# A Mamba-2 stage whose decay matrix is made from running sums that DMA broadcasts, in place of masked matrix products

## The chip, the cores and the metric

The kernel runs on one core of one Trainium2 chip. A core has five engines with instruction queues of their own: TensorE (PE, with its weight loads shown apart as PEld), VectorE (DVE), ScalarE (ACT), GpSimd (POOL) and SyncE (SP), which here issues nearly all DMA transfers. The metric is device time in microseconds (us) of one execution; a measurement of this kernel can tell a difference of about 0.2% from none.

## The reference

The reference is two transformer-like layers on x of 4 rows x 512 tokens x 512 channels, in float32. Each of four blocks first gates x with a bidirectional decaying sum over a side input (the "gates"; they depend on the side input and the condition, not on x, so they can be made ahead), then adds the block's output to x: a Mamba-2 mixer, a mixture of 8 experts (top 2), grouped attention with 16 heads, and a gated feed-forward with 1408 hidden channels.

The change lies in the Mamba-2 mixer. Cut to what matters, with 16 heads and a step size dt per token and head:

```python
dt = softplus(zxbcdt[..., -16:] + dt_bias)
dA = dt * (-exp(A_log))                      # negative, per token and head
dA_cs = cumsum(dA, axis=-1)                  # within a chunk of tokens
seg = dA_cs[..., :, None] - dA_cs[..., None, :]
Lmat = where(tri, exp(seg), 0.0)             # decay from token s to token l, l >= s
Y_diag = einsum('bcgls,bgHcls,bcsgHp->bclgHp', CB, Lmat, xdt)
decay_states = exp(dA_cs[..., -1:] - dA_cs)
Y_off = einsum('bclgn,bcgHpn,bgHcl->bclgHp', Cc, prev, exp(dA_cs))
```

After that follow a skip term, a gate silu(z), a root-mean-square norm and an output projection. The chunk length doesn't change the result; the kernel takes 128 tokens.

## The kernel before

Everything is float32. The stages run one after another: the first gates; the Mamba stage for the rows b = 0 to 3, in which the gates for later blocks and the routing of the experts are made as well; the experts; attention; the feed-forward. Instructions are written in one program order, and a scheduler of the framework orders each engine's queue from it; once built, each engine runs its queue strictly in order. `after(...)` holds back some instructions in that scheduling.

**A row of the Mamba stage** (from `start_row`, L961). `start_scan` computes dt and dA for the row's 512 tokens (`time_steps`, L865, a chain of small VectorE instructions with 64 columns: 4 tiles x 16 heads) and the B and C channels; `more_x` computes the other eight chunks of channels (`conv_chunk`, L915: four products on PE into one bank, one pass on ACT, three on VectorE). The next row's are made in tiles 2 and 3 of the row before. Then four tiles of 128 tokens follow.

**A tile** is put together by the loop at L1219. `start_tile` makes z (L994, 16 PE records of 512 columns) and its silu. `start_scores` (L1006) multiplies the tile's dA by three constant matrices (L1011: `tri_le` gives running sums, `tri_gt` the sums that are still to come, `ones` the total), takes exponentials of the 48 columns (`ex`), makes C times B (`cb`, masked with `tri_le` by VectorE, L1020) and a transpose of B (`bt`). `decays(u, hh)` (L1028) is called once for each half of the 16 heads. For each four heads it forms r, `tri_le` scaled by each head's dA: one GpSimd instruction for the first four (L1036), four ACT instructions for the other four (L1044). One product of `tri_gt` with r (L1046, `pseg`) then gives, for every pair of tokens, the sum of dA between them; ACT takes its exponential (`lm`, L1050) and VectorE multiplies by `cb` (L1051). The function also transposes x, scales it with dt (`xdt`) and with `dte` (`xde`), and starts the skip term. `outputs` (L1076) multiplies `lm` with `xdt` (L1087), adds the part from the state and updates the state. `squares`, `norm`, `turn`, `project`, `scale` and `add_x` finish the tile one tile later; `norm` is three Newton steps on one column, on GpSimd (L1128 to L1131).

**Gates in between.** `pump` (L367) moves a generator (`make_gates`, L337) some steps forward at about seven places of each tile. Each pair of channel chunks takes scans forward and backward on VectorE (L254, L260), with a product on ACT between them (`f`, L256), three VectorE passes (L271 to L275), and loads and stores on SP: `kt` (L235), `ek` (L240, L242), `ekv` (L244, L250), the finished gate `g` (L328). The buffer of a `kt` is free once L273 has read it. `apply_gate` (L375) and the routing of the experts (`route`, L488; its PE products at L512 and L555) take scratch tiles of a tag `th` with two buffers.

**Buffers.** `lm` has four buffers of four heads, r two, `cb` two. PE's results go to three tags of PSUM banks: `mm` (four), `tp` (two), `acc` (two); `pseg` takes an `mm`. At the start, before the first tile, some of these buffers are lent to the first gates.

## Time and profile before

| what | value |
|---|---|
| median of four runs | 2668.1 us (2663.76 to 2670.64) |
| profiled execution, its own time | 2674.81 us |
| its span, first to last instruction | 2673.1 us |
| busy: PE, DVE, ACT, POOL | 2514.9, 1434.4, 1004.3, 286.2 us |
| mean granted clock of PE | 0.974 |
| instructions | 24889 |

The profile is of one execution. An engine's busy time is the union of its instructions; records of PE overlap, as they are pipelined, so a mean duration of 600 ns is more than the time from one start to the next. A 512-column product in float32 appears as two records. PEclk is the clock that PE was granted, 1.00 being full speed. Waits say which engine sat idle before which line, until what ended it; "SPq" is SP's queue of DMA issues. By the lines in the profile, the first gates take 0 to about 60 us, the Mamba stage reaches from there to some 720 us (its tiles begin at 84 us), the experts end near 1240 us, and attention near 2210 us.

### The profile page before, as it was taken

The numbers are of one execution on the slowest core, as the hardware profiler recorded it, in microseconds if no ns is written. First come the engines' busy times: TensorE is split into PE (matmuls) and PEld (weight loads), VectorE is DVE, ScalarE is ACT, GpSimd is POOL, SyncE is SP. The second block draws the span as 40 slices with busy tenths as digits, with TensorE's granted clock in tenths as the row PEclk, the third lists the DMA queues.
The fourth block names the chain that finished last, engine by engine and source line by source line (L and its number), as shares of the span: only waits on it lengthen the run. The fifth ranks groups of instructions, "written<-read, shape, count | busy, mean of one in ns | idle before, by whom it ended". The sixth has DMA issues, their size and how long they took to land.

```text
span 2673.1 us, 24889 instructions
## 1 busy us (share of the span) xinstructions
PE 2514.9 (94%) x8398; PEld 1335.2 (50%) x8398; DVE 1434.4 (54%) x2777; ACT 1004.3 (38%) x2044; POOL 286.2 (11%) x403
## 2 busy tenths in 40 slices
PE   3999999999998999995999999999999999999999
PEld 1555555646644444442555555555555554444444
DVE  8788888896524565553675564555454441010110
ACT  4556545546321333331554544444444341010000
POOL 1141332223211112110000000000000000000000
PEclk9889899999999999997999999999999999999999
DMA  6121312212134487876120211111000003000000
GB/s 210 44 68 56 130 40 82 96 59 82 64 134 168 174 308 289 345 291 211 56 87 25 63 32 34 43 46 32 16 9 24 32 27 119 16 0 16 8 8 16
DMA packets 86111, 237.95 MB, mean 89 GB/s; under 512 B 9184, under 2 KB 18528, under 8 KB 75872
## 3 DMA queue, kind: packets, MB, share of 16 engines
q1 hardware_dynamic: 77440, 211.71, 22.9%
q0 software_dynamic: 6240, 20.45, 2.1%
q10 hardware_dynamic: 2304, 4.20, 0.4%
q8 instruction: 67, 1.10, 0.2%
q14 instruction: 60, 0.49, 0.1%
HBM read 268.05 MB, written 46.92 MB: 118 GB/s over the span
## 4 chain that ended last, share of the span: by engine, by line
PE 46%; DVE 4%; ACT 2%; DMA 1%; issue 1%; SPq 0%; POOLq 0%; ACTq 0%; DVEq 0%
PE pd L1521 8%; PE pq L1457 7%; PE pfu L1588 6%; PE pfo L1598 6%; PE pfg L1583 6%; PE pctx L1506 5%; PE psc L1474 3%; PE pv L1443 2%; PE ptp L1497 2%; PE pk L1435 2%; DVE nmax L1479 1%; DMA rr<-rows_o 1%; ACT pr L1484 1%; DVE psc L1477 1%; DVE den L260 0%
## 5 line engine op out<-in xcount | busy, mean ns | idle before, releaser
L1457 PE MATMUL pq<-h,wq 128*128 128x512 f32 x512 | 250.3, 605 | 7.5 <-ACT pr L1484 7.4
L1521 PE MATMUL pd<-cx,wd 128*128 128x512 f32 x512 | 222.4, 592 | 0.0
L923 PE MATMUL pc<-h,wxb 128*128 128x512 f32 x320 | 144.7, 610 | 37.7 <-DVE h L1199 37.7
L1593 DVE SCALAR_TENSOR_TENSOR hd<-pfu,cols,hd 128x512 f32<-128x512 f32 x44 | 33.0, 750 | 269.3 <-PE pfu L1588 269.2
L1477 DVE TENSOR_TENSOR psc<-psc,mask 128x128 f32<-128x128 f32 x256 | 71.9, 288 | 189.3 <-PE psc L1474 189.3
L1592 ACT ACTIVATE hd<-pfg,cols 128x512 f32<-128x512 f32 x44 | 30.2, 687 | 381.0 <-PE pfg L1583 381.0
L1484 ACT ACTIVATE pr<-psc,nmax 128x128 f32<-128x128 f32 (+3 forms) x256 | 135.1, 529 | 98.3 <-DVE nmax L1479 97.4
L1506 PE MATMUL pctx<-pT,v 128*128 128x512 f32 (+3 forms) x512 | 152.8, 441 | 7.3 <-ACT pT L1500 3.9
L1588 PE MATMUL pfu<-h,ffu 128*128 128x512 f32 x352 | 158.7, 592 | 0.9 <-DMA ffu<-in_upT 0.9
L1583 PE MATMUL pfg<-h,ffg 128*128 128x512 f32 x352 | 158.6, 592 | 0.0
L1521 PEld LDWEIGHTS pd<-cx,wd 128*128 128x128 f32 x512 | 96.1, 190 | 114.8 <-issue 110.5
L1474 PE MATMUL psc<-kT,qT 128*128 128x128 f32 (+3 forms) x512 | 151.4, 435 | 0.9 <-ACT pr L1484 0.7
L1598 PE MATMUL pfo<-hd,ffd 128*128 128x512 f32 x352 | 151.7, 592 | 0.0
L757 PE MATMUL po<-w,yT 128*128 128x512 f32 x312 | 141.6, 594 | 3.9 <-ACT yT L750 2.1
L724 PE MATMUL pg<-w,hT 128*128 128x512 f32 x312 | 141.6, 594 | 1.9 <-DMA w<-in_w1x 1.9
L1506 PEld LDWEIGHTS pctx<-pT,v 128*128 128x128 f32 x512 | 93.0, 189 | 96.8 <-issue 35.0
L735 PE MATMUL pn<-w,hT 128*128 128x512 f32 x312 | 140.4, 592 | 0.0
L1529 DVE TENSOR_TENSOR xr<-xr,pd 128x512 f32<-128x512 f32 x64 | 44.0, 688 | 174.8 <-PE pd L1521 174.8
L1479 DVE TENSOR_REDUCE nmax<-psc 128x1 f32<-128x128 f32 (+3 forms) x256 | 123.7, 485 | 2.7
L1497 PEld LDWEIGHTS ptp<-ident,pr 128*128 128x128 f32 x640 | 78.2, 143 | 86.8 <-issue 40.1
L994 PE MATMUL pz<-wzt,h 128*128 128x512 f32 x256 | 121.1, 614 | 0.0
L1457 PEld LDWEIGHTS pq<-h,wq 128*128 128x128 f32 x512 | 88.0, 194 | 66.1 <-issue 57.6
(292 smaller groups left out, 4314.0 us busy)
## 6 DMA issues: line engine op xcount, KB each, us to landing
w<-in_w1x SPq DMA_DIRECT2D x80, 1024.0 KB
w<-in_w2x SPq DMA_DIRECT2D x40, 1024.0 KB
wb<-in_b1x SPq DMA_DIRECT2D x40, 512.0 KB
kt<-in_fT SPq DMA_DIRECT2D x62, 256.0 KB
ek<-ek SPq DMA_DIRECT2D x62, 256.0 KB
ekv<-ekv SPq DMA_DIRECT2D x62, 256.0 KB
g<-num SPq DMA_DIRECT2D x30, 512.0 KB
h<-g SPq DMA_DIRECT2D x11, 1024.0 KB
```

Of the source, the lines that this page charges most:

```text
L724: nc.tensor.matmul(pg, lhsT=hT[:, k, :], rhs=self.w1[s][0][:, k, :], start=(k == 0), stop=(k == NC - 1))
L757: nc.tensor.matmul(po, lhsT=yT[:, j, :], rhs=self.w2[s][:, j, :], start=(j == 0), stop=(j == NI - 1))
L923: nc.tensor.matmul(pc, lhsT=wxb[:, k, m * P : (m + 1) * P], rhs=h[:, k, :], start=(k == 0), stop=(k == NC - 1),)
L1457: nc.tensor.matmul(pq, lhsT=u.wq[:, k, i * KVC : (i + 1) * KVC], rhs=u.h[:, k, :], start=(k == 0), stop=(k == NC - 1),)
L1474: nc.tensor.matmul(psc[:, :n], lhsT=qT[:, qi * P : n], rhs=u.kT[:, :n], start=True, stop=True)
L1479: nc.vector.tensor_reduce(nmax, psc[:, :n], AX.X, ALU.max, negate=True)
L1484: nc.scalar.activation(pr, psc[:, :n], AF.Exp, bias=nmax, accum_out=rsum)
L1506: nc.tensor.matmul(pctx[:, kj * P :], lhsT=u.v[:, kj, :], rhs=pT[:, kj, kj * P :], start=(kj == 0), stop=(kj == NT - 1),)
L1521: nc.tensor.matmul(po, lhsT=u.wd[:, i, m * P : (m + 1) * P], rhs=u.ctxT[i], start=(i == 0), stop=(i == HPG - 1),)
L1583: nc.tensor.matmul(pg, lhsT=wg[:, k, cs], rhs=h[:, k, :], start=(k == 0), stop=(k == NC - 1))
L1588: nc.tensor.matmul(pu, lhsT=wu[:, k, cs], rhs=h[:, k, :], start=(k == 0), stop=(k == NC - 1))
L1598: nc.tensor.matmul(po, lhsT=wdn[:, i, m * P : (m + 1) * P], rhs=hd[i], start=(i == 0), stop=(i == NFF - 1),)
```

## The change

The decay between two tokens is made from the row's running sums, by differences.

- `time_steps` now makes the three kinds of sums for the whole row at once (three products of 64 columns, in a `tp` bank), their exponentials `ex`, `dte`, and a copy `cs` of the running sums. `cs` is transposed on PE, copied (`csT`: one row of 128 tokens for each tile and head) and stored in DRAM (`cs_d`). Its scratch columns are one `th` tile instead of tiles of their own.
- `load_sums(w, t, hh)` is new. A DMA on SP's queue reads the eight heads' running sums of a tile (4 KB) and writes them to all 128 partitions of an `lm` tile (512 KB). It is called once for each `decays`, about half a tile ahead of it in program order.
- `decays` works in that tile. Eight ACT instructions form max(0, cs of the partition's token - cs of the column's token), one per head; one ACT instruction takes exp(-that) over 1024 elements; VectorE multiplies by `cb` in two halves, as before. r, L1036, L1044 and `pseg` are gone. For pairs that `cb` masks the maximum makes the factor 1.
- `lm` has three buffers of eight heads, `cb` has one; the lending of buffers at the start follows. `norm` takes two GpSimd instructions in place of four for each Newton step; `squares` three in place of two.

The diff, without the lending of buffers and the renaming of scratch tiles:

```diff
+    cs_d = [dr.tile([NT * NH, P], F32, name=f"cs{b}") for b in range(B)]
...
@@ time_steps
+            four = tmp.tile([P, 4, n], F32, tag="th", name="dtv")
+            v, z, w, w2 = (four[:, i, :] for i in range(4))
...
-            dA = sm.tile([P, NT, NH], F32, tag="dA", name="dA", bufs=2)
+            dA = w2.rearrange("p (t h) -> p t h", h=NH)
             nc.vector.tensor_tensor(
                 dA, dt, negA.unsqueeze(1).to_broadcast([P, NT, NH]), ALU.mult
             )
-            return dt, dA
+
+            pp = ps_tp("ppr")
+            for i, m in enumerate((tri_le, tri_gt, ones)):
+                nc.tensor.matmul(
+                    pp[:, i * n : (i + 1) * n], lhsT=m, rhs=dA.rearrange("p t h -> p (t h)"),
+                    start=True, stop=True,
+                )
+            ex = sm.tile([P, 3, NT, NH], F32, tag="ex", name="ex", bufs=2)
+            act(ex.rearrange("p a t h -> p (a t h)"), pp[:, : 3 * n], AF.Exp)
+            dte = sm.tile([P, NT, NH], F32, tag="dte", name="dte", bufs=2)
+            nc.vector.tensor_tensor(dte, dt, ex[:, 1], ALU.mult)
+
+            cs = sm.tile([P, n], F32, tag="cs", name="cs", bufs=2)
+            nc.vector.tensor_copy(cs, pp[:, :n])
+            pcs = ps_tp("pcs")
+            nc.tensor.transpose(pcs[:n, :P], cs, ident)
+            csT = four[:n, 0:2, :].rearrange("p i t -> p (i t)")
+            nc.vector.tensor_copy(csT, pcs[:n, :P])
+            nc.sync.dma_start(out=cs_d[b], in_=csT)
+            return dt, cs, ex, dte
...
@@ start_scores
             pp = ps_tp("pp")
-            for i, m in enumerate((tri_le, tri_gt, ones)):
-                nc.tensor.matmul(
-                    pp[:, i * NH : (i + 1) * NH], lhsT=m, rhs=w.dA[:, t, :], start=True, stop=True
-                )
...
-            u.ex = sm.tile([P, 3, NH], F32, tag="ex", name="ex", bufs=2)
-            act(u.ex.rearrange("p a h -> p (a h)"), pp[:, : 3 * NH], AF.Exp)
-            u.cb = sm.tile([P, P], F32, tag="cb", name="cb", bufs=2)
+            u.cb = sm.tile([P, P], F32, tag="cb", name="cb")
...
-            u.dte = sm.tile([P, NH], F32, tag="dte", name="dte", bufs=2)
-            nc.vector.tensor_tensor(u.dte, w.dt[:, t, :], u.ex[:, 1, :], ALU.mult)
+            u.ex, u.dte = w.ex[:, :, t, :], w.dte[:, t, :]
...
+        def load_sums(w, t, hh):
+
+            lm = w.lm[t, hh] = sm.tile([P, 8, P], F32, tag="lm", name="lm", bufs=3)
+            h0 = t * NH + hh * 8
+            nc.sync.dma_start(
+                out=lm.rearrange("p h l -> p (h l)"),
+                in_=cs_d[w.b][h0 : h0 + 8, :].rearrange("h l -> (h l)").partition_broadcast(P),
+            )
+
         def decays(u, hh):
 
             w, t = u.w, u.t
-            u.lm.append([])
-            for q in range(2):
-                h0 = hh * 8 + q * 4
-                r = sm.tile([P, 4, P], F32, tag="r", name="r", bufs=2)
-                if q == 0:
-                    nc.gpsimd.tensor_tensor(
-                        r,
-                        tri_le.unsqueeze(1).to_broadcast([P, 4, P]),
-                        w.dA[:, t, h0 : h0 + 4].unsqueeze(2).to_broadcast([P, 4, P]),
-                        ALU.mult,
-                    )
-                else:
-                    for i in range(4):
-                        nc.scalar.mul(r[:, i, :], tri_le, w.dA[:, t, h0 + i : h0 + i + 1])
-                pseg = ps_mm("pseg")
-                nc.tensor.matmul(
-                    pseg, lhsT=tri_gt, rhs=r.rearrange("p h l -> p (h l)"), start=True, stop=True
-                )
-                lm = sm.tile([P, 4, P], F32, tag="lm", name="lm", bufs=4)
-                act(lm.rearrange("p h l -> p (h l)"), pseg, AF.Exp)
+            lm = w.lm.pop((t, hh))
+            u.lm.append(lm)
+
+            for i in range(8):
+                h = t * NH + hh * 8 + i
+                nc.scalar.activation(
+                    lm[:, i, :], lm[:, i, :], AF.Relu, bias=w.cs[:, h : h + 1], scale=-1.0
+                )
+            lmf = lm.rearrange("p h l -> p (h l)")
+            act(lmf, lmf, AF.Exp, scale=-1.0)
+            for q in (slice(0, 4), slice(4, 8)):
                 nc.vector.tensor_tensor(
-                    lm, lm, u.cb.unsqueeze(1).to_broadcast([P, 4, P]), ALU.mult
-                )
-                u.lm[hh].append(lm)
+                    lm[:, q, :], lm[:, q, :], u.cb.unsqueeze(1).to_broadcast([P, 4, P]), ALU.mult
+                )
...
@@ norm
             for _ in range(3):
-                nc.gpsimd.tensor_tensor(q, rs, rs, ALU.mult)
-                nc.gpsimd.tensor_tensor(q, q, v, ALU.mult)
-                nc.gpsimd.tensor_scalar(q, q, -0.5, 1.5, ALU.mult, ALU.add)
-                nc.gpsimd.tensor_tensor(rs, rs, q, ALU.mult)
+                nc.gpsimd.tensor_scalar(q, rs, rs, hv, ALU.mult, ALU.mult)
+                nc.gpsimd.tensor_scalar(rs, q, 1.5, rs, ALU.add, ALU.mult)
...
@@ the loop over rows and tiles
-        w.dt, w.dA = time_steps(w.h, 0)
+        w.dt, w.cs, w.ex, w.dte = time_steps(w.h, 0)
+        load_sums(w, 0, 0)
...
         start_scores(u)
+        load_sums(w, 0, 1)
         decays(u, 0)
...
                 pump(1, last_gates)
+                if not last:
+                    load_sums(w, t + 1, 0)
+                elif b + 1 < B:
+                    load_sums(following, 0, 0)
                 decays(u, 1)
...
                 if nxt is not None:
+                    load_sums(w, nxt.t, 1)
                     decays(nxt, 0)
```

More of the change, by code (lines that the diff above doesn't have):

```diff
@@ L829, in lend, with lend_halves, take @@
             return take
-        four = (P, 4, P)
+        def lend_halves():
+            left = []
+            def take():
+                if not left:
+                    t = sm.tile([P, 8, P], F32, tag="lm", name="lm", bufs=3)
+                    left.extend(t[:, i : i + 4, :].rearrange("p a b -> p (a b)") for i in (0, 4))
+                return left.pop(0)
+            return take
         lent = [
@@ L834, in block_kernel @@
             {
[L835 removed]
+                "kt": lend("zs", 3), "ek": lend_halves(), "ekv": lend("xde", 2),
                 "f": lend("xdt", 2), "eu": lend("bc", 4), "den": lend("st", 1, (P, DI)),
@@ L845, in block_kernel @@
         x = {0: load_x(0)}
-        turned = []
+        turned, lend_turned = [], lend_halves()
         for cc in range(NC):
-            turned.append(lend("lm", 4, four)())
+            turned.append(lend_turned())
             act(turned[cc], x[0][:, cc, :], AF.Tanh, scale=0.5)
@@ L972, in start_scan @@
         def start_scan(w):
-            w.dt, w.dA = time_steps(w.h, w.b)
+            w.dt, w.cs, w.ex, w.dte = time_steps(w.h, w.b)
             w.Bc = conv_chunk(w.h, NDI)
@@ L1113, in squares @@
             if hh == 1:
[L1114 to L1117 removed]
+                u.v = sm.tile([P, 2], F32, tag="rv", name="rv", bufs=2)
+                v, hv = u.v[:, 0:1], u.v[:, 1:2]
+                nc.gpsimd.tensor_scalar(
+                    v, u.ss[:, 0:1], u.ss[:, 1:2], 1.0 / DI, ALU.add, ALU.mult
+                )
+                nc.gpsimd.tensor_scalar(hv, v, 1e-5, -0.5, ALU.add, ALU.mult)
+                nc.gpsimd.tensor_scalar(v, v, 1e-5, None, ALU.add)
         def norm(u):
[L1121 removed]
+            v, hv = u.v[:, 0:1], u.v[:, 1:2]
             rs = sm.tile([P, 1], F32, tag="rs", name="rs", bufs=2)
```

18 lines of the change are left out of this document (3 added, 15 removed).

## The prediction

> **What bounds the kernel now.** I read the chain that ended last first. It is PE from the attention stage on and reaches back only to 1214 us; nothing of it lies in the Mamba stage, where the whole change is. So that stage is read from busy time by stretches: the tiles of rows 0, 1 and 2 (84:212, 252:396, 436:580), the projections for the next row between them (212:252, 396:436) and row 3 (580:720).
>
> The columns are the stretch, its length, then busy us (and instructions) of PE, PEld, DVE, ACT and POOL, PE's granted clock, DMA share and GB/s:
>
> ```profile
> 84.00:212.00 128.00, 118.44 (x469) 70.80 (x468) 110.24 (x166) 81.19 (x152) 43.52 (x45) 0.90 0.20 64
> 212.00:252.00 40.00, 40.00 (x107) 18.69 (x106) 33.15 (x44) 19.53 (x37) 4.26 (x15) 1.00 0.11 40
> 252.00:396.00 144.00, 135.89 (x579) 84.99 (x578) 123.42 (x212) 81.79 (x158) 48.61 (x60) 0.93 0.27 88
> ...
> 436.00:580.00 144.00, 133.91 (x567) 83.27 (x567) 128.29 (x215) 79.59 (x156) 49.74 (x59) 0.93 0.28 92
> 580.00:720.00 140.00, 139.77 (x605) 83.47 (x604) 96.74 (x187) 74.20 (x152) 35.17 (x73) 1.00 0.21 68
> ```
>
> PE is 93 to 94% busy in the tiles of the first three rows, with DVE close behind (86 to 89%); in row 3, where few gates are left, PE alone is full. ACT stands at 53 to 63%, the DMA engines at 20 to 28%. Next, the waits within 84:720 (total us, times, longest):
>
> ```profile
> DVE cb L1020 <- ACT ex L123: 25.8, 9, 6.4
> DVE lm L1051 <- ACT lm L123: 22.5, 10, 6.9
> ```
>
> 48.3 us of DVE's idle time end with the decay chain: PE's `pp` and `pseg`, ACT's exponentials behind them. SP's own queue meanwhile stands at the loads of `kt`:
>
> ```profile
> SPq L235 <- DVE eu L273: 193.8, 25, 26.8
> ```
>
> Last, the groups by form within 84:720 (busy us, mean ns):
>
> ```profile
> L1046 PE MATMUL pseg<-r,tri_gt 128*128 128x512 f32 x128 | 65.1, 622 | 2.2 <-ACT r L1044 1.0 <-DVE st L1107 0.8 <-ACT lm L123 0.5
> ...
> L1051 DVE TENSOR_TENSOR lm<-lm,cb 128x512 f32<-128x512 f32 x64 | 53.5, 852 | 22.5 <-ACT lm L123 22.5
> ...
> L1044 ACT ACTIVATE r<-tri_le,dA 128x128 f32<-128x128 f32 x128 | 42.1, 393 | 0.0
> L1036 POOL TENSOR_TENSOR r<-tri_le,dA 128x512 f32<-128x512 f32 x32 | 41.5, 1296 | 267.7 <-PE pseg L1046 191.6 <-DVE dA L910 76.1
> ```
>
> The first, third and fourth disappear; the second stays as it is.
>
> **PE.** Records overlap, so I price them by start to start: in the timeline four `pseg` records take 1.88 us, 0.43 each. 128 x 0.43 = 55 us go. The three dA products of a tile (L1011, six records) take 0.66 us, 16 x 0.66 = 10.6 us; four groups, one per row with 64 columns in place of 16, and a transpose come in: 4 x 0.85 = 3.4 us. Net relief 62 us, 15.5 per row; at the 0.93 granted in the tiles of rows 1 and 2, 16.7.
>
> **ACT.** Four r products take 1.27 us, start to start 0.29; the differences have the same shape and also one value per partition, so 256 - 128 = 128 more cost 37 us. The exponentials move from 64 of 512 elements (two in 1.06 us) to 32 of 1024 (rec at L123: 1.06 us each): nothing. `ex` falls from 16 of 0.21 us to four. Net +35 us, 9 per row; ACT goes to 91 of 144 us, no bound. But the differences wait only for a DMA, not for PE, and in the changed instruction order they stand spread ahead of their use.
>
> **DVE.** `dte`, the copies of `cs` and `csT` and the 64 products with `cb` come to no change in sum. POOL's r products leave, and DVE runs slower beside POOL: `lm` takes 680 ns at the median but 852 in the mean, an excess of 64 x 0.17 = 11 us; the scans at L260 and L254 into num and L275, by mean less their duration before 84 us, add 8. POOL's r products are 41.5 of its 93 us of 512-element work (with L1098 and L1106), 45%, so 9 us of the 19 go, 2.2 per row.
>
> **Tiles of rows 0 to 2.** After this PE needs about 118 of 144 us and DVE 121 to 126: DVE becomes the busier. Today the stretch is 9 us longer than its busiest engine. If that stays, 144 becomes 132.5: 11.5 gained per row, close to the 12 (48.3 / 4) of decay-chain waits. From both sides: 2.2 if only the contention goes, 16.7 if PE's relief passes whole. I take 9, since longer runs of ACT will hold some gate products (L256) that DVE waits for: 3 x 9 = 27. **Row 3** is PE's own: 15.5 of relief, between 8 and 15.5 reach the end; I take 12, as routing answers (L512, L555) keep their place.
>
> **What is added.** At the start dA is ready at 90.1 us. Then follow PE until 92.4, copy, transpose and copy until 93.3, the store, the load, eight differences (2.4) and an exponential (1.06). Nearest rows: a store of `g` and the load that reads it are issued 3.4 us apart (145.03, 148.46); a load takes 2.6 to 5.9 us in the chain (`rr`) and 7.3 at the most (148.46 to its use at 155.75, with twice the bytes). With 3.4 and 3.5 the first diagonal products start near 104.4 where they started at 97.4. PE can do tile 1's z projections (7.0 us, at 103 today) meanwhile: a cost between 0 and 10, I take 4. `time_steps` now holds one of two `th` buffers until its store lands, and route's L553 stands four to six instructions behind on DVE in rows 1 and 2: 0 to 3.4 us each, I take 2 in all. The 32 loads write 16.8 MB; 46.7 MB cost 21.5% of the DMA engines in 60:720, so these cost about 8% more, beside engines at most 28% busy on average: nothing. The norm's shorter POOL chain ends 2.9 us of ACT waits and 3.5 of PE's at most: nothing taken. One `cb` buffer costs nothing, since DVE writes and reads it in order.
>
> **Sum.** -27 - 12 + 4 + 2 = -33 us. From the profiled execution's 2674.8 that gives 2642. Its own time is 6.7 us above the median of the four runs, so I forecast 2668 - 33 = **2635**. Later stages follow on data and are moved forward as they are.
>
> **A rule against it.** In 116:124 PE is busy 4.4 of 8 us and the next 8 us have a granted clock of 0.59; after 148:156 (4.3 busy) it is 0.50. Row 3, without gaps, has 1.00. The Trainium skill ("TensorE: Matmul & The Clock Gate", "Why this matters for your kernels") says the same: a gap over some 3 us drops the array to half rate until it has been busy again. This change makes PE the emptier engine. If the clock of the tiles fell from 0.93 to 0.88, an estimate on that rule, 118 us would become 125 per row: still level with DVE; only from there on would it eat the gain, and the sum by the rule is some 6 us smaller.
>
> **Rivals.** (A) DVE sets the tiles, and PE's relief turns into PE idle: DVE is over 86% busy, and its order is fixed. Three rows give 2.2 each, row 3 gives 8, less 6: about -9, 2659. Against it: the 48 us that DVE waits for this very chain. (B) All relief passes: 3 x 16.7 + 15.5 - 2 = -64, 2604. Against it: DVE would have to run at 97 to 100%. (C) Slower, by the new loads. SP works in order, and in the changed order 16 of the 32 loads stand behind a `kt` load that must wait for DVE's L273; such waits last 7.8 us on average, 26.8 at most. A late load stops ACT at its first difference, with `f`, `eu` and `zs` behind it, and DVE's backward scans behind those. A load is issued about half a tile (18 us) ahead and 7 us are needed for landing, differences and exponential, so waits over 11 us show. It decides once 33 / 16 = 2 us per such load are uncovered; at 3.5 us it is +56 - 33 = +23, 2691. Against it: the wait is for work that DVE has to do earlier anyway. (D) Gains and new waits cancel: 2668. That the products don't leave PE is excluded by the changed program, which has none of them.
>
> **Chances.** Forecast (-18 to -50) 0.46, A (-6 to -18) 0.17, B 0.11, D 0.08, C 0.18. Faster by over 0.2% (5.3 us, about what a measurement can tell from no change) 0.74, within it 0.08, slower 0.18. The range 2608 to 2674 leaves out half of B and most of C; taking in C whole would need 2691.
>
> **What would show it.** Right: L1046 and L1036 gone, PE busy in 84 to the stage's end near 545 us, DVE's waits for the decay chain gone, DVE over 90% busy in the tiles of rows 0 to 2, the stage's end (720 now) near 687. ACT waits for DMA at the differences, beyond 5 us in sum after the first tile, would speak for C; PE idle with a clock under 0.9 for A. Wrong from the start would be a broadcast load much slower than the 3.5 us taken.

## The result, and the profile after

| | before | changed |
|---|---|---|
| median of the runs | 2668.36 us (78 runs) | 2665.57 us (52 runs) |
| ratio, 95% interval | | 0.9986 [0.9978, 0.9993] |
| profiled execution: own time, span | 2674.81, 2673.1 us | 2666.71, 2665.0 us |
| busy PE, DVE, ACT, POOL | 2514.9, 1434.4, 1004.3, 286.2 | 2478.2, 1414.8, 1035.8, 252.4 us |
| mean granted clock of PE | 0.974 | 0.961 |

The change saves 0.14%, some 4 us, which is no change by the 0.2% of the prediction; 33 us were forecast. The profiled executions stand 6.4 and 1.1 us above these medians, so the two profiles differ by more (8.1 us) than the kernels. Below, a difference of 0.001 in a ratio is 2.7 us.

All that was to leave has left: PE and POOL are less busy, DVE too. The busy time by stretches of the changed kernel (length, then busy us and instructions of PE, PEld, DVE, ACT, POOL, then PE's granted clock, DMA share and GB/s):

```profile
84.00:212.00 128.00, 105.18 (x399) 64.46 (x398) 99.27 (x158) 86.67 (x175) 26.85 (x25) 0.84 0.29 95
252.00:396.00 144.00, 128.03 (x525) 85.86 (x524) 113.75 (x206) 85.52 (x171) 41.00 (x36) 0.83 0.32 106
436.00:580.00 144.00, 125.70 (x537) 83.24 (x536) 122.05 (x215) 86.66 (x174) 44.12 (x37) 0.87 0.37 119
580.00:720.00 140.00, 137.77 (x601) 83.34 (x600) 97.80 (x191) 84.66 (x175) 33.97 (x51) 0.98 0.32 106
```

The busy times and the clock tell it. In the tiles of rows 0 to 2, PE was busy for 118 to 136 us at a clock of 0.90 to 0.93; it is busy for 105 to 128 us at 0.83 to 0.87. PE and DVE both have more idle time than before, and yet the rows take as long: from its first z to that of row 3, the Mamba stage takes 519.4 us where it took 516.9, and the first z of row 3 starts at 602.95 us where it started at 600.02. Row 3 is clearly shorter (from its first z to its fourth 77.1 us, 89.2 before). The waits of the changed kernel in 84:720 (total us, times, longest):

```profile
DVE dtv L891 <- PE pdt L881: 17.4, 3, 8.6
...
DVE lg L471 <- PE pl L464: 14.7, 6, 4.5
...
DVE cb L1037 <- PE pp L1035: 11.0, 8, 2.5
...
ACT lm L1061 <- DMA lm<-cs: 9.1, 5, 4.8
...
DVE lm L1067 <- ACT lm L123: 4.8, 3, 2.6
```

The two waits for the decay chain (25.8 and 22.5 us before) are down to 11.0 and 4.8. But DVE now waits 17.4 us for `pdt`, the 32 short products of the next row's step sizes (6.7 before), and 14.7 us for `pl`, the short products of the experts' gate (4.8 before). Summed over all rows of this view, from 84 us to the start of row 3, DVE waits 51.6 us for PE (20.1 before) and 27.6 us for ACT (37.8 before): 85.7 us idle in all waits, 67.8 before. **PE has less to do and is late more often.** The groups of what was added (busy us, mean ns, then idle time before) are as priced:

```profile
L1061 ACT ACTIVATE lm<-lm,cs 128x128 f32<-128x128 f32 x256 | 80.9, 391 | 9.2 <-DMA lm<-cs 9.1
L1067 DVE TENSOR_TENSOR lm<-lm,cb 128x512 f32<-128x512 f32 x64 | 43.3, 709 | 4.8 <-ACT lm L123 4.8
```

The differences take 391 ns, the price taken. The multiplication by `cb` fell from 852 to 709 ns, 9 us of DVE's time. It follows POOL's r products: in the four kernels that keep them it takes 771 to 972 ns in the mean, in all others 681 to 709. In all, DVE's busy time in rows 0 to 2 fell by 15 us (446.9 to 432.0 us between the first z of row 0 and that of row 3), while its idle time grew by 17.

Where in a row the time comes and goes is seen from the stretches between first z products: tile 0 to tile 2 of row 1, tile 2 to the next row, and the same in row 2. Before:

```profile
239.43:305.81 66.38, 64.11 (x271) 39.97 (x269) 55.42 (x76) 43.87 (x87) 21.68 (x37) 0.92 0.28 91
305.81:418.49 112.68, 106.84 (x406) 61.47 (x405) 97.54 (x177) 54.21 (x100) 29.61 (x38) 0.95 0.20 68
418.49:484.22 65.73, 62.78 (x271) 38.91 (x269) 56.12 (x77) 44.39 (x88) 23.14 (x37) 0.95 0.28 93
484.22:600.02 115.80, 108.66 (x407) 62.42 (x406) 101.70 (x178) 55.16 (x102) 30.41 (x38) 0.94 0.24 75
```

After:

```profile
243.69:301.35 57.66, 54.94 (x239) 35.69 (x237) 47.48 (x70) 41.71 (x81) 14.28 (x23) 0.91 0.41 130
301.35:425.01 123.66, 110.41 (x390) 67.77 (x389) 101.66 (x183) 65.02 (x130) 31.26 (x23) 0.85 0.25 85
425.01:482.86 57.85, 55.01 (x238) 35.90 (x237) 47.16 (x70) 41.48 (x79) 14.27 (x23) 0.91 0.40 129
482.86:602.95 120.09, 104.63 (x389) 62.94 (x388) 104.90 (x185) 64.99 (x132) 33.08 (x23) 0.89 0.29 96
```

The first half of a row gains 8.7 and 7.9 us, about the forecast's 9 per row. The second half, where the experts are routed and the next row's step sizes are made, gives 11.0 and 4.3 us back, at a clock of 0.85 and 0.89.

The clock also goes with the time where nothing of the program differs. The executions of the changed kernel reach from 2650.0 us, at a mean granted clock of 0.969, to 2678.0 us at 0.958; over 54 executions a clock lower by 0.001 comes with 2.25 us more (correlation -0.94). By this slope the fall from 0.974 to 0.961 would be some 29 us, an estimate; between kernels it is no more than a hint, as the orders and the work differ.

### The profile page after: what moved, and what is told of

Its sections match the earlier page's. It is cut to its first block, busy times and chain, and to the rows that moved or that the text cites. A ratio compares the mean times of both kernels' runs of the same rounds, so it can differ in the third digit from the quotient of the medians.

```text
span 2665.0 us, 24542 instructions
## 1 busy us (share of the span) xinstructions
PE 2478.2 (93%) x8202; PEld 1325.9 (50%) x8202; DVE 1414.8 (53%) x2773; ACT 1035.8 (39%) x2128; POOL 252.4 (9%) x291
## 4 chain that ended last, share of the span: by engine, by line
PE 46%; DVE 4%; ACT 2%; DMA 1%; issue 1%; SPq 0%; POOLq 0%; ACTq 0%; DVEq 0%
PE pd L1544 8%; PE pq L1480 7%; PE pfu L1611 6%; PE pfo L1621 6%; PE pfg L1606 6%; PE pctx L1529 5%; PE psc L1497 3%; PE pv L1466 2%; PE ptp L1520 2%; PE pk L1458 2%; DVE nmax L1502 1%; DMA rr<-rows_o 1%; ACT pr L1507 1%; DVE psc L1500 0%; DVE den L260 0%
## 5 line engine op out<-in xcount | busy, mean ns | idle before, releaser
L947 PEld LDWEIGHTS pc<-h,wxb 128*128 128x128 f32 x320 | 62.4, 198 | 117.5 <-issue 75.8
```

Source lines behind the costliest of these rows:

```text
L947: nc.tensor.matmul(pc, lhsT=wxb[:, k, m * P : (m + 1) * P], rhs=h[:, k, :], start=(k == 0), stop=(k == NC - 1),)
```

## The experiments

Four theories came up on the way. **T**: the sums, made for a whole row at its end, put a wait there that costs the gain (the first four expectations set it against rivals R1, that PE's relief is worth little in rows 0 to 2, and R2, that the falling clock eats it). **V**: VectorE, in its fixed order, sets rows 0 to 2. **K**: in the freed time PE stands idle, its clock halves, and the short products behind the gap, which DVE waits for, take twice as long. **O**: the scheduler makes other queue orders of the changed text, and these happen to be worse. Each was stated before its runs. All ratios are to the kernel before; the last column is the difference to the changed kernel's 0.9986, in us, which is uncertain by about 5 us in most rows. Except where orders are said to be held or the same, the scheduler also made other queue orders of each changed text.

| run | ratio, 95% interval | us to changed |
|---|---|---|
| late sums | 0.9958 [0.9942, 0.9974] | -7 |
| dummy products everywhere | 1.0008 [0.9998, 1.0017] | +6 |
| before, no `pseg` product | 0.9965 [0.9948, 0.9983] | -6 |
| before, sums for a row | 1.0034 [1.0021, 1.0046] | +13 |
| half the `cb` products | 0.9875 [0.9859, 0.9892] | -30 |
| late sums, long dummies in rows 1, 2 | 0.9857 [0.9840, 0.9873] | -34 |
| late sums, tiny dummies in rows 1, 2 | 0.9916 [0.9900, 0.9932] | -19 |
| late sums, dt after B and C | 0.9949 [0.9934, 0.9963] | -10 |
| order of long dummies, tiny ones | 0.9889 [0.9867, 0.9911] | -26 |
| order of tiny dummies, long ones | 0.9963 [0.9948, 0.9977] | -6 |
| order of dummies everywhere, tiny ones | 0.9955 [0.9938, 0.9972] | -8 |
| norm as before | 0.9953 [0.9934, 0.9971] | -9 |
| gap before `pl` filled | 0.9960 [0.9943, 0.9978] | -7 |
| four gaps filled | 0.9949 [0.9932, 0.9967] | -10 |
| late sums, norm as before | 0.9910 [0.9890, 0.9930] | -20 |
| the same, long dummies in rows 1, 2 | 0.9882 [0.9859, 0.9906] | -28 |
| before, short `pseg` products | 0.9971 [0.9956, 0.9986] | -4 |
| short `cb` products | 0.9937 [0.9921, 0.9952] | -13 |

### Sums late, and sums early in the kernel before

In the changed kernel the row sums move from the end of `time_steps` (tile 2) to the start of the row's last tile:

```diff
@@ time_steps
+            return dt, dA
+
+        def row_sums(dt, dA, b):
             pp = ps_tp("ppr")
...
@@ the loop, last tile of a row
                 elif b + 1 < B:
+                    f = following
+                    f.cs, f.ex, f.dte = row_sums(f.dt, f.dA, b + 1)
                     load_sums(following, 0, 0)
```

> The changed kernel with the row's sums (three products, ex, dte, cs, the transpose and the store) taken out of time_steps and made one tile later, at the start of the row's last tile. Theory T (the tail): made right behind dA, these products put PE's ordered queue behind VectorE's chain for dA in tiles 2 and 3 of rows 0 to 2; PE idles 4 to 6 us each time, its clock halves, and what the early tiles won is given back there. T expects 10 to 25 us less than the changed kernel (2641 to 2656). Rival R1 (order): rows 0 to 2 are set by VectorE's ordered queue and its answers from ACT, so that freeing PE is worth nothing there, wherever the sums stand; R1 expects 2661 to 2670.

Measured: 0.9958, a median of 2653.4 us, 7 us less than the changed kernel. PE's waits ahead of `ppr` fall from 13.8 to 2.6 us.

In the kernel before, the three dA products, `ex` and `dte` are made at the end of `time_steps` for the whole row; the `pseg` products stay:

```diff
-            return dt, dA
+            pp = ps_tp("ppr")
+            for i, m in enumerate((tri_le, tri_gt, ones)):
...
+            return dt, dA, ex, dte
```

> The kernel before with only the row's sums of the change: the three dA products, ex and dte once for a row at the end of time_steps, its scratch in a th tile, one cb buffer; r and pseg stay. T expects PE's waits for dA in tiles 2 and 3 here too: 5 to 15 us more than before, though 7 us of PE work go. R1 expects 0 to 6 us less than before.

Measured: 1.0034. The kernel before gets 9 us **slower** although 7 us of PE's work go. That lies in T's range, but the trace doesn't show T's wait as the reason: PE waits for dA ahead of `ppr` for 3.9 us in all, and in the profiled execution (2670.6 us) rows 1 and 2 are shorter than before (176.9 and 177.0 us for 179.1 and 181.5). Both runs also have queue orders of their own, and the same text in another order differs by as much (below). So T's wait is seen, but its size in time isn't shown by itself. It is at most a part: with late sums rows 1 and 2 still give 5.4 and 7.2 us back in their second halves (118.1 and 123.0 us).

### TensorE work put back, and taken from the kernel before

Each call of `decays` in the changed kernel gets two products of the old size that nobody reads:

```diff
             for q in (slice(0, 4), slice(4, 8)):
+                pseg = ps_mm("pseg")
+                nc.tensor.matmul(
+                    pseg, lhsT=tri_gt, rhs=skip[:, q, :].rearrange("p h l -> p (h l)"),
+                    start=True, stop=True,
+                )
```

> The changed kernel with the 64 removed products of 512 columns put back as idle work: the same weights, a constant on the right, a result that nobody reads. If PE's relief counts everywhere (the forecast's view), 35 to 50 us more than the changed kernel (2700 to 2716). If it counts in row 3 alone (R1), 10 to 15 us more (2676 to 2681). If the idle work also keeps PE's clock up in rows 0 to 2 (R2, the clock), less than 10 us more, at most 2675.

And the kernel before without its products (ACT takes the exponential of r itself):

```diff
-                pseg = ps_mm("pseg")
-                nc.tensor.matmul(
-                    pseg, lhsT=tri_gt, rhs=r.rearrange("p h l -> p (h l)"), start=True, stop=True
-                )
...
-                act(lm.rearrange("p h l -> p (h l)"), pseg, AF.Exp)
+                act(lm.rearrange("p h l -> p (h l)"), r.rearrange("p h l -> p (h l)"), AF.Exp)
```

> The kernel before without the product that makes pseg: ACT takes the exponential of r itself, so the decays between tokens are other numbers; all else stays. It shows PE's relief of 55 us alone, without new loads, more ACT work or row sums. If PE counts in all rows: 30 to 45 us less than before (2623 to 2638). If only in row 3 (R1): 8 to 15 us less (2653 to 2660). T expects the first.

Measured: 55 us of PE work put back cost 6 us; 55 us taken away bring 9. In the first, rows 1 and 2 even got shorter than the changed kernel's (first z to first z 172.4 and 173.8 us, 181.3 and 177.9 there), and row 3 longer (88.4 for 77.1). So the forecast's relief is not there to be had in rows 0 to 2 (R1; T had expected 30 to 45 us from the second run), and work nobody needs made two rows faster (for R2, later K).

### VectorE's load

In the changed kernel, half the multiplications by `cb` are left out:

```diff
-            for q in (slice(0, 4), slice(4, 8)):
+            for q in (slice(0, 4),):
                 nc.vector.tensor_tensor(
```

> The changed kernel without the multiplication by `cb` for the second four heads of each half (32 of the 64 instructions of L1067): their diagonal part then lacks the mask and C times B. VectorE loses 32 x 0.68 to 0.85 = 22 to 27 us, 24 of the 32 in rows 0 to 2. Theory V (VectorE, in its fixed order, sets the tiles of rows 0 to 2): 24 x 0.7 = 17 us less than the changed kernel's ratio of 0.9986, so 0.990 to 0.994. Theory K (what holds rows 0 to 2 are exchanges between VectorE and a TensorE whose clock falls in the gaps): less VectorE work leaves as many exchanges, so under 8 us less, 0.996 to 0.9986. Theory O (rows 0 to 2 differ by the queue orders that the scheduler happens to make): anything between, no steady relation.

Measured: 0.9875, 30 us for 22 to 27 us of DVE's work. More than V's 17; but the scheduler made other orders of this text, so it is tried again below with orders held.

### Dummies in rows 1 and 2, long and tiny

Late sums, with the two dummy products only in rows 1 and 2, once with 512 columns, once with 16:

```diff
+                if w.b in (1, 2):
+                    pseg = ps_mm("pseg")
+                    nc.tensor.matmul(
+                        pseg[:, :512], lhsT=tri_gt,
+                        rhs=skip[:, q, :].rearrange("p h l -> p (h l)"),
+                        start=True, stop=True,
+                    )
```

> The version with late sums, with dummy products of 512 columns (two for each call of decays) in rows 1 and 2 only: 32 of them, 27 us of TensorE time that nobody uses. In the run with dummies everywhere, rows 1 and 2 were 9 and 4 us shorter than the changed kernel's from first z to first z, and only rows 0 and 3 longer. Theory K: the dummies keep the clock up and rows 1 and 2 get 5 to 13 us shorter, so 0.991 to 0.994 against 0.9958 without them. Theory V: TensorE has the time to spare, so nothing changes, 0.995 to 0.997. If TensorE's time counts after all: 14 to 27 us longer, over 1.001.

> The same with dummies of 16 columns: the same places in the program, some 2 us of TensorE time in all, too little to hold a clock. Theory K: within 3 us of the version with late sums (0.9958), the clock of the tiles no higher than there. Theory O: the new instructions alone change the queue orders, and the time moves as far as with the long dummies, in either direction, with the same clock.

Measured: long 0.9857, tiny 0.9916, none 0.9958. 27 us of useless work make the kernel 27 us faster, twice what K expected, and 2 us of it make it 11 us faster, where K expected nothing. The stretches of row 1 with long dummies, as above:

```profile
232.90:295.88 62.98, 60.74 (x258) 36.95 (x257) 53.25 (x77) 46.28 (x91) 17.44 (x24) 0.95 0.39 124
295.88:401.29 105.41, 103.65 (x402) 59.20 (x400) 93.88 (x177) 60.97 (x120) 20.10 (x23) 0.97 0.29 97
```

PE does more and the first half is 5.3 us longer than the changed kernel's; the second half is 18.3 us shorter, at a clock of 0.97 in place of 0.85. But tiny dummies cannot hold a clock, and helped too: the queue orders of the two differ from that without dummies. K and O are not yet told apart.

### The step sizes behind B and C

```diff
         def start_scan(w):
-            w.dt, w.dA = time_steps(w.h, w.b)
             w.Bc = conv_chunk(w.h, NDI)
             w.Cc = conv_chunk(w.h, NDI + 1)
+            w.dt, w.dA = time_steps(w.h, w.b)
```

> The version with late sums, with the step sizes of the next row computed behind its B and C channels instead of ahead of them (two lines of start_scan change places). VectorE waited 8.1 us for the 32 short products of `pdt`, once in each of rows 0 to 2; now it has six passes over B and C to do meanwhile. If such exchanges set rows 0 to 2 (K): 3 x 3 to 3 x 6 us less than the version with late sums, 0.989 to 0.992. If VectorE's amount of work does (V): no change, 0.995 to 0.997.

Measured: 0.9949, 2 us under late sums and within the error of it, where K had expected 9 to 18. Inconclusive: DVE's waits for `pdt` are down from 16.0 to 8.6 us, as meant, but those for `pl` stay (16.3 us for 14.8), and rows 1 and 2 take 177 us each (176 and 180 with late sums).

### Orders held: order against clock

To hold the orders, a program is built twice: the first build gives each engine's order, the second adds an edge from each instruction to the next of its engine, which orders and doesn't wait. In the traces, each such run has the instructions of its model in the same order on every engine. So the dummies' length and the queue orders can be crossed.

```diff
     with tile.TileContext(nc) as tc:
         block_kernel(tc, aps, out)
+        if order is not None:
+            traced = {i.name: i for i in nc.cur_bb.bb.instructions}
+            for names in order.values():
+                names = [n for n in names if n in traced]
+                for a_, b_ in zip(names, names[1:]):
+                    tc.add_manual_dep(
+                        traced[b_], a_,
+                        mybir.DependencyInfo(mybir.DependencyClass.NoSync, mybir.DependencyReason.DATA),
+                        reason="issue_after",
+                    )
...
+    first, _ = build(inputs, 512)
...
+    nc, arrays = build(inputs, 16, order)
```

> Every engine's queue holds its instructions in exactly the order of the version with long dummies in rows 1 and 2 (pinned by edges that only order, without waits), but the dummies have 16 columns: 27 us less TensorE work in rows 1 and 2, nothing else. Theory K (the long dummies hold the clock up): the time goes back to that of the tiny dummies or of none, 0.991 to 0.996. Theory O (the queue orders that the scheduler made with long dummies are the better ones): as fast as with long dummies, or faster by what TensorE saves, 0.980 to 0.9857.

> The other way round: the queue orders of the version with tiny dummies, with dummies of 512 columns. Theory K: about as fast as the scheduled version with long dummies, 0.984 to 0.988, the clock of rows 1 and 2 near 0.96. Theory O: no faster than the tiny ones (0.9916), and up to 27 us slower where TensorE is late, 0.991 to 1.002.

> The changed kernel in exactly the queue orders of the run with dummies everywhere (ratio 1.0008), with dummies of 16 columns. Rows 0 and 3, which the dummies made some 15 us longer, win that back in both theories. K: rows 1 and 2, which had become 13 us shorter, go back to the changed kernel's length: 0.998 to 1.001 in all. O: they keep it, 0.991 to 0.996, and then the changed kernel's give-back is in the orders that the scheduler made for it.

| late sums | order made for long | order made for tiny |
|---|---|---|
| long dummies | 0.9857 | 0.9963 |
| tiny dummies | 0.9889 | 0.9916 |

Read down the columns: with the same orders, 27 us of PE work cost 12 us in one and **save** 9 in the other. Read across: with the same work, the order is worth 28 us or 7. The 28 and the 12 are clear of the error, the 9 only just and the 7 hardly; the interaction of 21 us is uncertain by 9. The clock of rows 1 and 2 goes the same way: long dummies raise it to 0.96 from 0.92 and 0.93 in the first order, and leave it at 0.91 and 0.89, tiny ones at 0.92 and 0.93, in the second. Neither theory stands alone: the first run (0.9889) lies between O's range and K's, the second (0.9963) in O's. The third, the changed kernel's text with tiny dummies in another order, is 8 us faster with almost the same work (O's range): the scheduler's order is a term of that size by itself, and it is no property of the change that one could have forecast.

### The norm as before

```diff
             for _ in range(3):
-                nc.gpsimd.tensor_scalar(q, rs, rs, hv, ALU.mult, ALU.mult)
-                nc.gpsimd.tensor_scalar(rs, q, 1.5, rs, ALU.add, ALU.mult)
+                nc.gpsimd.tensor_tensor(q, rs, rs, ALU.mult)
+                nc.gpsimd.tensor_tensor(q, q, v, ALU.mult)
+                nc.gpsimd.tensor_scalar(q, q, -0.5, 1.5, ALU.mult, ALU.add)
+                nc.gpsimd.tensor_tensor(rs, rs, q, ALU.mult)
```

(and `squares` with two instructions in place of three)

> The changed kernel with squares and norm as before (twelve and two small GpSimd instructions in place of six and three, for each tile); the orders of TensorE, VectorE and ScalarE are the same. The forecast took the new norm at nothing: then 0.9975 to 0.9997, as the changed kernel's 0.9986. In the changed kernel's profile its six steps take 1.3 to 2.4 us each, where the twelve took some 0.5 us; if the norm now ends later and that reaches the scaling of y, this run is 3 to 10 us faster, 0.995 to 0.9975.

Measured: 0.9953, 9 us faster than the changed kernel. The orders of PE, DVE and ACT are the same up to one DVE instruction in row 3 (the norm's first step, one place earlier), so the two traces can be laid side by side. Between the first z of tiles 1 and 2 of row 2, the changed kernel takes 34.6 us, this run 30.3. In the timelines (start, us, instruction, in brackets the idle time ahead and what ended it), the changed kernel:

```profile
457.71 0.36 PE L464 MATMUL pl<-gw,h 128*128 128x8 f32 x2 [1.95 <-issue]
...
459.27 1.81 PE L1102 MATMUL pyd<-xdt,lm 128*128 128x64 f32 x8
...
462.25 2.25 PE L464 MATMUL pl<-gw,h 128*128 128x8 f32 x10
...
464.54 0.17 DVE L471 TENSOR_TENSOR lg<-pl,rows 128x16 f32<-128x16 f32 x1 [3.61 <-PE pl L464]
```

The run with the norm as before:

```profile
452.73 0.36 PE L464 MATMUL pl<-gw,h 128*128 128x8 f32 x2 [1.54 <-issue]
...
453.82 1.00 PE L1102 MATMUL pyd<-xdt,lm 128*128 128x64 f32 x8
...
455.40 1.23 PE L464 MATMUL pl<-gw,h 128*128 128x8 f32 x10
...
456.67 0.17 DVE L471 TENSOR_TENSOR lg<-pl,rows 128x16 f32<-128x16 f32 x1 [0.72 <-PE pl L464]
```

In this place the clock makes the difference. `squares` has three instructions on POOL in place of two; DVE's first step of the norm waits 0.67 us for them in place of 0.30, so all behind it on DVE is 0.4 us late, `h` too, and PE stands idle for 1.95 us ahead of `pl` in place of 1.54. In the one case PE has half its clock from 458.28 to 468.52 us, and the products behind the gap run at half the pace (8 `pyd` in 1.81 us for 1.00, ten `pl` in 2.25 for 1.23); DVE waits 3.61 us for them instead of 0.72. In the other the clock stays full.

But the longer gap isn't shown as the reason. In row 1 of the same run the same gap of 1.54 us is followed by half clock, too:

```profile
274.20 0.36 PE L464 MATMUL pl<-gw,h 128*128 128x8 f32 x2 [1.54 <-issue]
...
277.92 2.25 PE L464 MATMUL pl<-gw,h 128*128 128x8 f32 x10
...
280.20 0.17 DVE L471 TENSOR_TENSOR lg<-pl,rows 128x16 f32<-128x16 f32 x1 [2.79 <-PE pl L464]
```

And in row 2 of both kernels a gap of 1.86 us is followed by full clock, with a wait of 1.00 us. Of the eight gaps ahead of `pl` in rows 1 and 2 of the two kernels, all of 1.5 to 2.0 us, five are followed by half clock. The clock in these traces changes only in steps of 3.41 us, so where a gap falls among them may decide as much as its length. So the cost of the norm as a whole, 9 us, is measured; how it comes about is not shown.

### Gaps filled, orders held

If K is the cause, work in the gap must make the kernel faster with nothing else moved. The changed kernel in its own orders, with products that nobody reads ahead of `pl` (rows 1 and 2), and then also ahead of `pcnt`, `ppr` and `ptok`:

```diff
         pl = ps_tp("pl")
+        for _ in range(3 * (b < 2)):
+            nc.tensor.matmul(
+                pl[:, 256:].rearrange('p (a l) -> p a l', l=P), lhsT=tri_gt,
+                rhs=ident.unsqueeze(1).to_broadcast([P, 2, P]), start=True, stop=True,
+            )
```

> The changed kernel in its own queue orders, pinned, with three products of 256 columns (1.3 us) that nobody uses ahead of the expert gate's products (`pl`) in rows 1 and 2, where TensorE stands idle for 1.9 us: 12 products, 5 us of work. Theory K (such a gap halves the clock, and the exchange behind it pays): VectorE's waits of 3.6 to 4.5 us for `pl` fall under 1 us, 1.5 to 3 us won at each of four places, 0.9940 to 0.9970 against the changed kernel's 0.9986. If the gap is only idle time: 0.9980 to 1.0005.

> The same, also ahead of `pcnt` (three products), `ppr` (eight, behind the wait for the step sizes) and `ptok` (six) in the tail of the rows: 54 products, 23 us of work, all queue orders those of the changed kernel. Theory K: the clock of the tails rises from 0.85 to 0.9 toward 0.95, and 10 to 20 us go, 0.9910 to 0.9950. If the gaps are only idle time, or the fillers delay what stands behind them: 0.9980 to 1.0050.

Measured: 0.9960 and 0.9949, both within K's ranges, the second at its edge. The tile `pl` in the window 84:600 (ns of one: least, median, most; then what waited for it), of the changed kernel:

```profile
L464 PEld LDWEIGHTS pl<-gw,h x64: 186/333/338, 276.4 to 496.7; 128*128 128x128 f32 x64
L464 PE MATMUL pl<-gw,h x64: 175/346/363, 276.4 to 496.7; 128*128 128x8 f32 x64
...
  DVE lg L471: 12.3, 4
```

With the gap filled:

```profile
L468 PEld LDWEIGHTS pl<-gw,h x64: 186/192/192, 275.3 to 485.7; 128*128 128x128 f32 x64
L468 PE MATMUL pl<-gw,h x64: 172/256/277, 275.5 to 485.8; 128*128 128x8 f32 x64
...
  DVE lg L475: 5.5, 4
```

The same products take 256 ns at the median in place of 346, their weight loads 192 in place of 333, and DVE waits 6.8 us less for them, close to the 7 us measured (uncertain by 5). With `pl` filled, none of the four places has half clock, in either run; in the changed kernel three have. Filling the three other gaps adds 18 us of work and 3 us of gain, which the intervals don't separate from none.

### Late sums and the norm together, and the fastest version

The two edits shown above, without and with long dummies in rows 1 and 2:

> The version with late sums (0.9958) with the norm as before as well (alone 0.9953). If the two costs are separate they add: 0.9910 to 0.9935, which would make the decays from running sums worth some 20 us without their two companions. If both are the same lost gap: 0.9945 to 0.9965.

> The version with late sums and long dummies in rows 1 and 2 (0.9857) with the norm as before. If the costs are separate: 0.9810 to 0.9840. If the norm's cost is the clock's, and the dummies hold the clock already: 0.9845 to 0.9870.

Measured: 0.9910, so the two gains add up (7 + 9, 20 measured), and without its two companions (the early sums and the new norm) the change is worth 24 us against the kernel before, in this queue order. The norm's part holds with the orders of late sums, which are the same in both: 13 us, uncertain by 7. With dummies 0.9882, no better than 0.9857 with the new norm (same orders again): with the clock of rows 1 and 2 at 0.96, the norm's cost isn't seen. The version with late sums and long dummies, 0.9857 [0.9840, 0.9873], is the fastest run here; late sums with the norm as before is the fastest of the full kernels without useless work.

### What the two large terms are worth, orders held

The kernel before with its `pseg` products cut to 16 columns (ACT reads these again and again), and the changed kernel with half its `cb` products cut to 4 of 128 columns:

```diff
-                    pseg, lhsT=tri_gt, rhs=r.rearrange("p h l -> p (h l)"), start=True, stop=True
+                    pseg[:, :16], lhsT=tri_gt, rhs=r.rearrange("p h l -> p (h l)")[:, :16],
...
+                n = P if q.start == 0 else 4
                 nc.vector.tensor_tensor(
-                    lm[:, q, :], lm[:, q, :], u.cb.unsqueeze(1).to_broadcast([P, 4, P]), ALU.mult
+                    lm[:, q, :n], lm[:, q, :n], u.cb[:, :n].unsqueeze(1).to_broadcast([P, 4, n]),
+                    ALU.mult,
                 )
```

> The kernel before in exactly its own queue orders, with the `pseg` products cut to 16 of their 512 columns (ScalarE's exponentials read those columns again and again; the decays are other numbers): 64 products, some 50 us of TensorE work less, nothing else changed. The forecast's step (9 per row in rows 0 to 2 and 12 in row 3 from relief of this size) would give 30 to 39 us: 0.985 to 0.989. If relief counts only in row 3, where TensorE is full, and its gaps cost clock elsewhere: 6 to 14 us, 0.9945 to 0.998.

> The changed kernel in exactly its own queue orders, with the multiplication by `cb` for the second four heads of each half cut to 4 of 128 columns per head (the rest keeps decays without mask and C times B): 32 instructions of 0.68 us become some 0.15, 17 us less of VectorE work, 13 of it in rows 0 to 2. If VectorE's amount of work sets those rows: 10 to 17 us less than the changed kernel's 0.9986, 0.992 to 0.995. If the exchanges with TensorE do: under 5 us, 0.9965 to 0.9990.

Measured: 50 us of PE's work are worth 8 us (0.9971), with 4 to 12 us as the interval. 32 instructions of DVE shortened from 682 to 219 ns in the mean, 15 us, are worth 13 (0.9937), uncertain by 5. In the first, from first z to first z, rows 1 and 2 have 160 and 167 us of PE's work (171 and 171 before) and 152 and 159 of DVE's (153 and 158), and the decay chain's waits stay (23.7 and 18.1 us): rows 0 to 3 get 4.2, 5.4, 0.9 and 4.8 us shorter in the profiles. So DVE's time in the changed kernel counts for far more than PE's in the kernel before, as V would have it. That it counts one to one is not shown: in the second run's profile 9.2 us of the gain are in row 1, where DVE has 3.5 us less work and waits 5 us less for PE, and rows 0 and 2 gain 0.1 and 1.2 us. The change itself took 15 us of DVE's work from rows 0 to 2, and they got no shorter.

## Why the prediction was wrong

**What was right.** The durations: 391 ns for a difference; the contention of r with the products by `cb` (9 us); ACT off the path at 87 of 144 us. The waits for the decay chain went, from 48.3 to 15.8 us. Row 3 gains 12.1 us, as taken, and dummies put back there cost 11.3 (88.4 us for 77.1). But the kernel before gains only 4.8 us in that row from its short products, so PE's relief alone isn't shown to be the whole of it, and the match of the number has some luck in it. The start is as late as taken within 3 us (first diagonal products at 107.4 us, 104.4 taken), and PE fills it as taken, with tile 1's z at 103.1 us; what of the 4 us taken for it reaches the end wasn't measured by itself. ACT waits 9.1 us for the loads in five places, 9.0 of it after the first tile. That is above the 5 us that the prediction named as a sign for rival C, and far under the 2 us for each of 16 at which C would decide.

**The step that failed is "Tiles of rows 0 to 2"**: three times 9 us, by the rule that a stretch stays 9 us longer than its busiest engine. From first z to first z these rows got 2.5 us longer, not 27 shorter. With orders held, PE's relief is worth 8 us in all, row 3 included. DVE's time does count, and the change takes 15 us from it in these rows, more than twice what was taken, but the waits that went were replaced: DVE waits 31.5 us more for PE and 10 less for ACT. So a stretch does not keep its distance to the busiest engine. That PE's relief turns into idle time was rival A's mechanism, and its sign (PE idle, clock under 0.9) is there. A gave 2.2 us per row, and without its two companion edits the change gets about 4: in the profile of late sums with the norm as before, row 3 starts 12.7 us earlier than before and is 12.2 us shorter, near the 24 us measured.

**The clock was taken too small, and in the wrong place.** The prediction priced a fall from 0.93 to 0.88 as 7 us of PE's own time, "still level with DVE". It fell to 0.83 to 0.87, and the price is more than PE's time: short products run at half pace, and DVE waits behind each. With orders held this is shown where the gaps ahead of `pl` are filled (7 us). The Trainium skill ("TensorE: Matmul & The Clock Gate", "What's actually happening") lets the clock fall after an idle window of about 3.4 us; here it fell after gaps of 1.5 to 2.0 us between short products in five of eight places, so a price by gaps over 3 us, as in the prediction, counts too few of them. In the traces of all kernels here, up to 760 us, each step of 3.41 us at full clock in which PE was busy for less than 40% was followed by half clock (102 of 102), and of those with 40 to 60% most were (88 of 139); the clock came back only after steps with 80% or more. So the share of a step that is busy says more than the length of a gap.

**Two terms were taken at nothing or nearly.** "The norm's shorter POOL chain: nothing taken" costs 9 us. "`time_steps` now holds a `th` buffer: 2 us" looked at the buffer and not at PE's queue: the row's sums stand behind DVE's chain of step sizes, PE waits for it (up to 5.4 us ahead of `ppr`, 1.7 ahead of `pcs`), and late sums win 7 us back, in another queue order. Together 16 to 20 us. Rival D, "gains and new waits cancel", has come true, with waits it didn't name.

**What stays open** is how much of the rest is the scheduler's order. Nearly the same text is 8 us faster in another order, and with dummies the orders differ by 7 to 28 us. Why one order is better wasn't found; that its effect depends on what PE does in the gaps is shown by the crossed runs, with their interaction of 21 us. How the norm's 9 us come about is open, and so is how much of the late sums' 7 us is order. That the fall of the clock costs time in the other gaps (`pdt`, `ppr`) as it does at `pl` is argued from the trace, as filling those ahead of `pcnt`, `ppr` and `ptok` showed no clear gain.

## What to carry to other kernels

Before counting relief of an engine as gain, cut its work in place with every queue order held: 50 us of an apparently full PE were worth 8 here, 15 us of DVE 13. Where two engines exchange short results, a gap in PE can cost more than its length, when what comes back through it runs at half the clock; look for the short products behind each gap before making PE emptier. And take a change apart into its companions: without two small ones, this one was worth 24 us in place of 4.

## What the runs showed of the hardware

- Gaps of 1.5 to 2.0 us in PE ahead of short products were followed by half clock in five of eight places of two kernels, for some 10 us each, by gaps of 1.54 us too; 12 products of 256 columns put into such gaps brought the weight loads behind them from 333 back to 192 ns at the median.
- An instruction of one column on POOL, beside DVE, takes from 340 ns to 2.3 us in one and the same form (L1146). In the changed kernel, over the window 84:720 (busy us, mean ns):

```profile
L1146 POOL TENSOR_SCALAR rq<-rs,rv 128x1 f32<-128x1 f32 x42 | 47.2, 1123 | 11.9 <-DVE rs L1141 9.1
L1147 POOL TENSOR_SCALAR rs<-rq,rs 128x1 f32<-128x1 f32 x42 | 35.2, 838 | 4.4
```

Two such instructions with values per partition take 1.96 us in the mean, the four of the old form 2.27 (560, 607, 518 and 583 ns, in the run with the norm as before): half the instructions save 14% of the time. The Trainium skill ("SBUF — State Buffer", "SBUF: two separate sides") says that a GpSimd instruction and a DVE instruction with two inputs from SBUF lock each other out for a whole instruction; steps of 1.1 to 2.3 us, the length of one or two DVE passes (0.7 to 1.3 us each), agree with that, but no run here shows the lock by itself.
- Useless work can pay: with the orders held, 27 us of products that nobody reads made the kernel 9 us faster in one order, and 12 us slower in another.
